# The first part of a LoRA-MoE layer with its operands swapped: tokens as TensorE's weights, 512 outputs streaming, results turned by VectorE and ScalarE

## The chip, the cores and the metric

The kernel runs on one NeuronCore of a Trainium2 chip. The metric is device time in microseconds, the median of several executions. Everything is fp32; the trace shows each fp32 matmul as two MATMUL instructions.

## What is computed

Eight sequences of 256 tokens with 1024 features go through three steps:

```python
w = cond_weight[ids]                                # one 1024 x 1024 matrix for each sequence
y = einsum('bsi,boi->bso', x, w)                    # part one
p = softmax(y @ router_W.T + router_b)              # 15 columns; the top 8 stay
w8 = sum of the kept p by expert_map                # 8 experts
h = y @ A.T                                         # 8 experts x rank 16 = 128 columns
out = x + (y @ base_W.T + base_b) + 2 * (h * w8) @ B
```

The matrix of a sequence differs from the next one's, so part one has eight products of 256 x 1024 by 1024 x 1024. Part two has one matrix, `base_W`, for all 2048 tokens.

## The kernel before

Both parts use the Winograd form of a 2 x 2 block product: seven block products in place of eight, and sums and differences of the blocks on VectorE.

**Part one** is a loop over the eight sequences `b`. The input of a sequence is cut into two halves of features (4 x 128 each) and two halves of tokens (128 each); its matrix into two halves of features and two of outputs (512 each). `load(b + 1)` brings the next sequence's tokens and the four quarters of its matrix (`a11`, `a12`, `a22`, `a21`, 1 MB each) with SP's queue into the tiles `x` and `wt` (eight buffers). VectorE makes the differences of the tokens in `turns` (`t1`, `t2`, `t4`), the sum `s1` in `first_sum`, and `s2`, a new `a21` and `s4` in `other_sums`, always for the next sequence, during the present one. TensorE runs seven blocks for each sequence: `a11`, `a12`, `s1`, `s2`, `a21`, `s4`, `a22` by their token blocks. A block is 16 matmuls of 128 x 128 weights, taken from the matrix, with 128 tokens streaming (`block`, L241). Its result lies in PSUM in `pa`, `pb` or `pc`, 2 buffers each, outputs on partitions and tokens along the free side. Some blocks accumulate on a bank that was read before (`s2` and `a22` on `pa`, `s4` on `pc`). ScalarE copies `pa` and `pc` out after their first use (L382, L394, L396) and takes the last block (L420); VectorE adds the others (L386, L408, L424). The results go straight into `ys`, where part two wants them: features on partitions, tokens along the free side.

Between the blocks of sequence `b` stands the routing of sequence `b - 1`: `project` (16 matmuls of 143 columns, L105), the softmax, the top 8 and the weights on VectorE (`weigh`), and `turn`, two TensorE transposes and a ScalarE copy that bring the weighted `h` into `hwTs`. After the loop the last `turn`, `project` and `weigh` follow.

`prepare_load(b)` loads a piece of `base_W` into `spare`; `prepare(b - 1)` makes the sums that part two needs (4 VectorE instructions for the first four pieces, 8 for the others) and writes them to DRAM (`left_raw`, `left_sum`). `load_left(n)` reads the left operands of product `n` of part two back. In the last iteration the order on SP is: `load_left` for the first product, `prepare(7)`'s two writes, `load_left` for the second product.

**Part two** takes the tokens in two groups of four sequences. Each group has seven outer products (`seven`), and each outer product is again seven blocks (`product`, L468), here 4 matmuls of 256 columns in a block, with the `up` terms of the LoRA part (L477) in four of the seven outer products. A queue of small VectorE steps (`soon`, `later`) is worked off between the blocks, two at a time. Group 0 is products 0 to 6, group 1 is products 7 to 13.

The order on TensorE, VectorE, ScalarE and SP is the order of the program text (`manual_schedule`). Every engine works through its instructions in that order.

Of the kernel before, what the change touches and what calls it, by code (L numbers as in the profile page):

```python
# [28 lines left out]
def kernel(  # L29
# [57 lines left out]

    ys = [
        ypool.tile([P, 2, 2, 2, 2, 2, S], F32, name=f"y{g}") for g in range(B // GB)
    ]  # L90
    hwTs = [const.tile([P, 2, 2, S], F32, name=f"hwT{g}") for g in range(B // GB)]
# [4 lines left out]
    def project(b, ar_sb, rpool, ps_h, order=(0, 1)):  # L96

        y = ys[b // GB]
        th, bi = b % GB // 2, b % 2
        h = rpool.tile([P, NTT, ER], F32, name="h")  # L100
        lg = rpool.tile([P, NTT, N], F32, name="lg")
        ph = ps_h.tile([P, NTT, ER + N], F32, name="ph")
        for j in order:
            for k in range(KC):
                nc.tensor.matmul(  # L105
                    ph[:, j],
                    lhsT=y[:, k // KH, th, k % KH // 2, bi, k % 2, ts(j, P)],
                    rhs=ar_sb[:, k, :],
                    start=(j == order[0] and k == 0),
                    stop=(k == KC - 1),  # L110
                    skip_group_check=True,
                )
        nc.scalar.copy(h, ph[:, :, :ER])  # L113
        nc.vector.tensor_add(  # L114
            lg, ph[:, :, ER:], rb.unsqueeze(1).to_broadcast([P, NTT, N])
        )
        mx = rpool.tile([P, NTT], F32, name="mx")
        nc.vector.tensor_reduce(mx, lg, AX.X, ALU.max)
        nc.vector.tensor_sub(lg, lg, mx.unsqueeze(2).to_broadcast([P, NTT, N]))
        ex = rpool.tile([P, NTT, N], F32, name="ex")  # L120
        nc.scalar.activation(ex, lg, AF.Exp)
        return h, ex

    def weigh(h, ex, route, rpool, hwpool):

        den = rpool.tile([P, NTT], F32, name="den")
        nc.vector.tensor_reduce(den, ex, AX.X, ALU.add)
        rden = rpool.tile([P, NTT], F32, name="rden")
        nc.vector.reciprocal(rden, den)
        pr = rpool.tile([P, NTT, N], F32, name="pr")  # L130
        nc.vector.tensor_mul(pr, ex, rden.unsqueeze(2).to_broadcast([P, NTT, N]))
        top = rpool.tile([P, NTT, 8], F32, name="top")
        rest = rpool.tile([P, NTT, N], F32, name="rest")
        for j in range(NTT):
            nc.vector.max(out=top[:, j, :], in_=pr[:, j, :])
        for j in range(NTT):
            nc.vector.match_replace(
                out=rest[:, j, :],
                in_to_replace=top[:, j, :],
                in_values=pr[:, j, :],  # L140
                imm_value=0.0,
            )

        kept = rpool.tile([P, NTT, N], F32, name="kept")
        nc.vector.tensor_sub(kept, pr, rest)
        w = rpool.tile([P, NTT, E], F32, name="w")
        for j in range(NTT):
            kr = rpool.tile([P, E, N], F32, name="kr")
            nc.vector.tensor_mul(
                kr, route, kept[:, j, :].unsqueeze(1).to_broadcast([P, E, N])  # L150
            )
            nc.vector.tensor_reduce(w[:, j, :], kr, AX.X, ALU.add)
        hw = hwpool.tile([P, NTT, ER], F32, name="hw")
        nc.vector.tensor_mul(
            hw.rearrange("p j (e r) -> p (j e) r", r=R),
            h.rearrange("p j (e r) -> p (j e) r", r=R),
            w.rearrange("p j e -> p (j e)").unsqueeze(2).to_broadcast([P, NTT * E, R]),
        )
        return hw
# [45 lines left out]
    with ExitStack() as phase:  # L205
        xpool = phase.enter_context(tc.tile_pool(name="x", bufs=2))
        mpool = phase.enter_context(tc.tile_pool(name="m", bufs=1))
        cpool = phase.enter_context(tc.tile_pool(name="c1", bufs=1))
        rpool = phase.enter_context(tc.tile_pool(name="route", bufs=2))
# [8 lines left out]

        em_f = cpool.tile([P, N], F32, name="em_f")
        route = cpool.tile([P, E, N], F32, name="route")  # L220

        def constants():
            nc.sync.dma_start(rb, router_b.to_broadcast([P, N]))
            nc.sync.dma_start(em_i, emap.to_broadcast([P, N]))
            nc.sync.dma_start(bb, base_b)
            nc.sync.dma_start(ar_sb.rearrange("p k n -> p (k n)"), ar)
            nc.vector.tensor_sub(bb[:, KH:], bb[:, KH:], bb[:, :KH])
            nc.vector.tensor_copy(em_f, em_i)
            for e in range(E):
                nc.vector.tensor_scalar(  # L230
                    route[:, e, :], em_f, float(e), SCALING, ALU.is_equal, ALU.mult
                )

        ar_sb = cpool.tile([P, KC, ER + N], F32, name="ar_sb")

        def block(acc, left, right, first, k_outer=False):
            order = [(m, k) for m in range(KH) for k in range(KH)]
            if k_outer:
                order.sort(key=lambda mk: mk[1])
            for n, (m, k) in enumerate(order):  # L240
                nc.tensor.matmul(  # L241
                    acc[:, m // 2, m % 2, :],
                    lhsT=left[:, k, ts(m, P)],
                    rhs=right[:, k, :],
                    start=(first and n == 0),
                    stop=(k == KH - 1),
                    skip_group_check=True,
                )

# [109 lines left out]
        waiting = None  # L359
        for b in range(B):  # L360
            last = b == B - 1

            def out(oh, th):
                return ys[b // GB][:, oh, b % GB // 2, :, b % 2, :, ts(th, P)]
# [10 lines left out]
            pa = ps.tile([P, 2, 2, P], F32, name="pa")  # L375
            pb = ps.tile([P, 2, 2, P], F32, name="pb")
            pc = ps.tile([P, 2, 2, P], F32, name="pc")
            m1 = mpool.tile([P, 2, 2, P], F32, name="m1")
            u2 = mpool.tile([P, 2, 2, P], F32, name="u2")
            m5 = mpool.tile([P, 2, 2, P], F32, name="m5")  # L380
            block(pa, q["a11"], b11, True, b == 0)
            nc.scalar.copy(m1, pa)  # L382
            if waiting:
                turn(*waiting)
            block(pb, q["a12"], b21, True, b == 0)
            nc.vector.tensor_add(out(0, 0), pb, m1)  # L386
            if b == 0:
                pd = ps.tile([P, 2, 2, P], F32, name="pb")
                block(pd, q["a22"], t4, True, True)
                nc.scalar.copy(out(1, 0), pd)  # L390
            if not last:
                nt1, nt2, nt4 = turns(x)
            block(pc, q["s1"], t1, True, b == 0)
            nc.scalar.copy(m5, pc)  # L394
            block(pa, q["s2"], t2, False)
            nc.scalar.copy(u2, pa)  # L396
            if b > 0:
                h, ex = project(b - 1, ar_sb, rpool, ps_h)
            if not last:
                first_sum(nq)  # L400
            if b == 0:
                block(pc, q["s4"], b22, False)
                block(pa, q["a21"], b12, False)
                nc.vector.tensor_add(out(1, 1), pa, m5)
                nc.vector.tensor_add(out(1, 0), pa, out(1, 0))
            else:
                block(pa, q["a21"], b12, False)
                nc.vector.tensor_add(out(1, 1), pa, m5)  # L408
                hw = weigh(h, ex, route, rpool, rpool)
                waiting = b - 1, hw  # L410
                block(pc, q["s4"], b22, False)
                if last:
                    nc.vector.tensor_add(out(0, 1), pc, u2)
                    left[0] = load_left(lefts[0])
                    terms = [step() for step in differences(ys[0][:, 0, 0])]
                    prepare(b)
                block(pa, q["a22"], t4, False)
                if last:
                    left[1] = load_left(lefts[1])
                nc.scalar.copy(out(1, 0), pa)  # L420
            if not last:
                other_sums(nq)
                q, t1, t2, t4 = nq, nt1, nt2, nt4
                nc.vector.tensor_add(out(0, 1), pc, u2)  # L424
# [5 lines left out]


        turn(*waiting)
        nh, nex = project(B - 1, ar_sb, rpool, ps_h, (1, 0))
        waiting = B - 1, weigh(nh, nex, route, rpool, const)

    with ExitStack() as phase:
# [3 lines left out]
        xpool = phase.enter_context(tc.tile_pool(name="x2", bufs=6))  # L443
        vpool = phase.enter_context(tc.tile_pool(name="v", bufs=1))
# [123 lines left out]
        for g in range(B // GB):  # L568
            y, hw = ys[g], hwTs[g]
# [3 lines left out]
            v = vpool.tile([P, 2, 2, 2, S], F32, name="v")  # L573
# [6 lines left out]
            def load_x(*r):  # L580
                xs[r] = xpool.tile([P, 2, S], F32, name="xt")
# [62 lines left out]
            for n, (right, base, into, done, *up_hw) in enumerate(seven):  # L644
# [5 lines left out]
                else:  # L650
                    follows = None if end else ys[g + 1][:, 0, 0]
# [25 lines left out]
                if end and n == 6:  # L677
# [4 lines left out]
                    )  # L682
                if here + 2 < len(lefts):
# [10 lines left out]
                if here == 0:  # L694
                    turn(*waiting)
# [65 lines left out]
```

## Time and profile before

| what | value |
|---|---|
| median of three runs | 442.53 us (442.32 to 443.61) |
| the profiled execution, its own time | 444.51 us |
| its span, first to last instruction | 442.7 us |
| TensorE busy (matmul) | 436.4 us, 99% |
| VectorE busy | 303.1 us, 68% |
| ScalarE busy | 40.3 us, 9% |
| mean granted TensorE clock | 0.996 |
| DMA | 106.19 MB, mean 240 GB/s |

The span is cut in time by the stages: part one's first block starts at 7.42 us, its last block ends at about 238.0 us, the turn and projection of sequence 7 end at 242.1 us, and part two runs from there to the end. A busy share is an average over stages that differ. A row of the timeline gives start, duration, engine, line, operation, output<-input, shapes and a count, and in brackets the idle time before it and what ended it. Matmul ends are modelled and overlap a little, so the time of a block is read from the start of one to the start of the next.

### The profile page before, as it was taken

The page shows a single profiled execution, that of the slowest core. Times are in us where ns is not written, and L with a number is a line of the kernel's source. Part 1 is how long each engine was busy: PE and PEld are TensorE (multiplying, and loading weights), DVE is VectorE, ACT ScalarE, POOL GpSimd, SP SyncE. Part 2 cuts the span into 40 slices and gives each one's busy share as a digit, 9 for nine tenths or more (in the row PEclk, how much of TensorE's full clock was granted, in tenths as well). Part 3 has the DMA queues.
Part 4 walks back from the last instruction along what each step waited for, and adds up shares of the span by engine and source line. Part 5 has one row for each costly group of instructions (what it writes and reads, how often), then busy time and mean ns, then how long its engine had stood idle before and what let it go on. Part 6 is the DMA issues. An engine that isn't in the chain of part 4 may idle for free.

```text
span 442.7 us, 7249 instructions
## 1 busy us (share of the span) xinstructions
PE 436.4 (99%) x2998; PEld 411.8 (93%) x2998; DVE 303.1 (68%) x516; ACT 40.3 (9%) x89; POOL 0.7 (0%) x6
## 2 busy tenths in 40 slices
PE   7999999999999999999999999999999999999997
PEld 6999999999999999999999888888888888888886
DVE  2678696582872976949719957756497867755594
ACT  1110101111011110110111200000200200000200
POOL 0000000000000000000000000000000000000000
PEclk8999999999999999999999999999999999999999
DMA  8997977668588777884280966730977726921843
GB/s 316 362 389 285 329 267 285 236 260 287 210 283 244 271 266 284 286 305 148 99 330 1 331 263 238 318 133 14 353 277 235 279 95 222 359 94 45 312 145 139
DMA packets 32786, 106.19 MB, mean 240 GB/s; under 512 B 3058, under 2 KB 6898, under 8 KB 29554
## 3 DMA queue, kind: packets, MB, share of 16 engines
q1 hardware_dynamic: 32466, 104.69, 65.0%
q10 hardware_dynamic: 288, 1.05, 0.6%
q8 instruction: 23, 0.38, 0.3%
q14 instruction: 9, 0.07, 0.0%
HBM read 84.49 MB, written 21.23 MB: 239 GB/s over the span
## 4 chain that ended last, share of the span: by engine, by line
PE 93%; DVE 5%; DMA 1%; issue 1%; SPq 0%
PE pa L241 25%; PE pa L468 20%; PE pc L241 12%; PE pc L468 10%; PE pb L241 7%; PE ph L105 6%; PE pb L468 5%; PE pc L477 3%; PE pb L477 2%; PE pa L477 1%; DMA wt<-in_wq_dram 1%; DVE tt L184 1%; PE pe L468 1%; DVE y L620 0%; PE pt L201 0%
## 5 line engine op out<-in xcount | busy, mean ns | idle before, releaser
L468 PE MATMUL pa<-tt,wt 128*128 128x256 f32 x324 | 78.0, 379 | 0.1
L468 PEld LDWEIGHTS pa<-tt,wt 128*128 128x128 f32 x324 | 61.4, 190 | 8.9 <-DVE u L498 0.5
L241 PE MATMUL pa<-x,wt 128*128 128x128 f32 x512 | 61.3, 280 | 1.9 <-DMA wt<-in_wq_dram 1.9
L241 PEld LDWEIGHTS pa<-x,wt 128*128 128x128 f32 x512 | 60.0, 196 | 2.0 <-issue 2.0
L241 PE MATMUL pa<-tt,wt 128*128 128x128 f32 x480 | 56.0, 275 | 0.0
L241 PEld LDWEIGHTS pa<-tt,wt 128*128 128x128 f32 x480 | 54.8, 192 | 0.0
L114 DVE TENSOR_TENSOR lg<-ph,rb 128x30 f32<-128x30 f32 x8 | 1.5, 188 | 50.1 <-ACT h L113 50.1
L105 PE MATMUL ph<-ar_sb,y 128*128 128x143 f32 x256 | 32.7, 284 | 0.0
L105 PEld LDWEIGHTS ph<-ar_sb,y 128*128 128x128 f32 x256 | 31.8, 190 | 0.0
L241 PE MATMUL pc<-tt,wt 128*128 128x128 f32 x256 | 29.9, 275 | 0.0
L241 PE MATMUL pb<-x,wt 128*128 128x128 f32 x256 | 29.9, 275 | 0.0
L241 PE MATMUL pc<-x,wt 128*128 128x128 f32 x256 | 29.9, 275 | 0.0
L241 PEld LDWEIGHTS pc<-tt,wt 128*128 128x128 f32 x256 | 29.2, 192 | 0.0
L241 PEld LDWEIGHTS pc<-x,wt 128*128 128x128 f32 x256 | 29.2, 192 | 0.0
L241 PEld LDWEIGHTS pb<-x,wt 128*128 128x128 f32 x256 | 29.2, 192 | 0.0
L468 PE MATMUL pc<-tt,wt 128*128 128x256 f32 x112 | 27.8, 379 | 0.0
L332 DVE TENSOR_TENSOR wt<-wt 128x2048 f32<-128x2048 f32 (+1 forms) x9 | 18.4, 2050 | 8.9 <-DMA wt<-in_wq_dram 8.8
L468 PE MATMUL pc<-y,wt 128*128 128x256 f32 x96 | 24.0, 379 | 0.0
L468 PE MATMUL pb<-y,wt 128*128 128x256 f32 x96 | 24.0, 379 | 0.0
L468 PEld LDWEIGHTS pc<-tt,wt 128*128 128x128 f32 x112 | 21.2, 190 | 3.0
L468 PE MATMUL pa<-y,wt 128*128 128x256 f32 x92 | 21.8, 379 | 0.0
L591 DVE TENSOR_TENSOR q<-q,xt 128x512 f32<-128x512 f32 x31 | 21.3, 686 | 0.5
(117 smaller groups left out, 489.0 us busy)
## 6 DMA issues: line engine op xcount, KB each, us to landing
wt<-in_wq_dram SPq DMA_DIRECT2D x28, 1024.0 KB, 5.1
wt<-left_raw SPq DMA_DIRECT2D x14, 1024.0 KB, 5.3
wt<-left_sum SPq DMA_DIRECT2D x14, 768.0 KB, 7.6
xt<-in_xr_dram SPq DMA_DIRECT2D x32, 256.0 KB, 6.4
out_dram<-q SPq DMA_DIRECT2D x31, 256.0 KB, 2.2
x<-in_xq_dram SPq DMA_DIRECT2D x7, 1024.0 KB, 4.8
wt<-in_wq_dram SPq DMA_DIRECT2D x8, 512.0 KB, 6.8
spare<-in_bq_dram SPq DMA_DIRECT2D x4, 1024.0 KB, 5.1
```

The lines of the kernel that those rows point to most:

```text
L105: nc.tensor.matmul(ph[:, j], lhsT=y[:, k // KH, th, k % KH // 2, bi, k % 2, ts(j, P)], rhs=ar_sb[:, k, :], start=(j == order[0] and k == 0 ...
L114: nc.vector.tensor_add(lg, ph[:, :, ER:], rb.unsqueeze(1).to_broadcast([P, NTT, N]))
L184: nc.vector.tensor_sub(t[n], x, y)
L241: nc.tensor.matmul(acc[:, m // 2, m % 2, :], lhsT=left[:, k, ts(m, P)], rhs=right[:, k, :], start=(first and n == 0), stop=(k == KH - 1), ...
L332: nc.vector.tensor_add(q["s1"][:, h], q["a21"][:, h], q["a22"][:, h])
L468: nc.tensor.matmul(acc[mi][:, mi, :], lhsT=left[:, 2 * k + mi, :], rhs=right[:, k, :], start=(first and k == 0 and (mi == 0 or acc[0] is n ...
L477: nc.tensor.matmul(acc[mi][:, mi, :], lhsT=up[:, ts(mi, P)], rhs=hw, start=False, stop=True, skip_group_check=True,)
L591: add(q, q, x)
```

## The change

In part one the two operands change places. A block is now 4 matmuls: 128 x 128 tokens are the weights, and 512 outputs of the matrix stream. The result of a block has tokens on partitions and 512 outputs along the free side, in four staging areas (`m0` for output half 0, `m1` for output half 1, two token halves each). To bring it into the layout of `ys`, `flip` has VectorE transpose each 128 x 512 piece in blocks of 32 x 32, and `moves` has ScalarE copy the blocks across partitions: 16 copies of 32 partitions x 256 elements for each of `m0` and `m1`. The copies of `m0` are issued after its second flip, the copies of `m1` at the start of the next sequence: eight before the copy of `pa`, eight after it (`behind`). The last 16 copies of sequence 7 lie between the blocks of part two's first product.

The block of `s4` now stands before `a21`, and `project` between `a21` and `a22`. `other_sums` stands after the routing steps, and the last flip, which reads `pa` directly in place of ScalarE's copy, after `other_sums`. `project` and `weigh` are one function that returns four steps. The projection of the last sequence is moved behind part two's second product, its `turn` behind the third; the `turn` of sequence 6 is behind the first product. In the last iteration `prepare(7)` is behind the last flip. Staging, routing values and the tile `v` of part two share one tile, `late`; four of the six `xt` places are the staging areas.

```diff
-    def project(b, ar_sb, rpool, ps_h, order=(0, 1)):
+    late = const.tile([P, 4 * OH + 2 * KC * S // 2 + 512], F32, name="late")
+    lo = 4 * OH
+    ms = late[:, :lo].rearrange("p (o h f) -> p o h f", o=2, h=2)
+    v = late[:, lo : lo + 8 * S].rearrange("p (i j k t) -> p i j k t", i=2, j=2, k=2)
...
+    def project(b, ph, order=(0, 1)):
...
+        return [logits, softmax, top, weigh], (b, hw)
...
-        def block(acc, left, right, first, k_outer=False):
-            order = [(m, k) for m in range(KH) for k in range(KH)]
-            if k_outer:
-                order.sort(key=lambda mk: mk[1])
-            for n, (m, k) in enumerate(order):
+        def block(acc, left, right, first):
+
+            for k in range(KH):
                 nc.tensor.matmul(
-                    acc[:, m // 2, m % 2, :],
-                    lhsT=left[:, k, ts(m, P)],
-                    rhs=right[:, k, :],
-                    start=(first and n == 0),
+                    acc,
+                    lhsT=right[:, k, :],
+                    rhs=left[:, k, :],
+                    start=(first and k == 0),
                     stop=(k == KH - 1),
                     skip_group_check=True,
                 )
+
+        def flip(half, of):
+
+            nc.vector.transpose(half, of)
+
+        def moves(b, oh, m):
+
+
+            y = ys[b // GB][:, oh, b % GB // 2, b % 2].rearrange(
+                "p q k (h a j) -> p (q k) h a j", h=2, a=4
+            )
+            m = m.rearrange("p h (q r j) -> p q h r j", q=KH, r=4)
+            return deque(
+                (
+                    lambda a=a, r=r: nc.scalar.copy(
+                        y[32 * r : 32 * r + 32, :, :, a, :], m[32 * a : 32 * a + 32, :, :, r, :]
+                    )
+                )
+                for r in range(4)
+                for a in range(4)
+            )
+
+        def run(steps, n=None):
+            for _ in range(len(steps) if n is None else min(n, len(steps))):
+                steps.popleft()()
...
-            block(pa, q["a11"], b11, True, b == 0)
-            nc.scalar.copy(m1, pa)
+            m0, m1 = ms[:, 0], ms[:, 1]
+            block(pa, q["a11"], b11, True)
+            run(behind, 8)
+            nc.scalar.copy(m0[:, 0], pa)
             if waiting:
                 turn(*waiting)
-            block(pb, q["a12"], b21, True, b == 0)
-            nc.vector.tensor_add(out(0, 0), pb, m1)
+            run(behind)
+            block(pb, q["a12"], b21, True)
+            nc.vector.tensor_add(m0[:, 0], pb, m0[:, 0])
+            flip(m0[:, 0], m0[:, 0])
...
-            block(pc, q["s1"], t1, True, b == 0)
-            nc.scalar.copy(m5, pc)
+            block(pc, q["s1"], t1, True)
+            nc.scalar.copy(m1[:, 1], pc)
             block(pa, q["s2"], t2, False)
-            nc.scalar.copy(u2, pa)
-            if b > 0:
-                h, ex = project(b - 1, ar_sb, rpool, ps_h)
+            nc.scalar.copy(m0[:, 1], pa)
             if not last:
                 first_sum(nq)
+            block(pc, q["s4"], b22, False)
+            nc.vector.tensor_add(m0[:, 1], pc, m0[:, 1])
+            flip(m0[:, 1], m0[:, 1])
+            run(moves(b, 0, m0))
+            block(pa, q["a21"], b12, False)
+            nc.vector.tensor_add(m1[:, 1], pa, m1[:, 1])
+            flip(m1[:, 1], m1[:, 1])
+            if last:
+                left[0] = load_left(lefts[0])
+                terms = [step() for step in differences(yv[0][:, 0, 0])]
             if b == 0:
-                block(pc, q["s4"], b22, False)
-                block(pa, q["a21"], b12, False)
-                nc.vector.tensor_add(out(1, 1), pa, m5)
-                nc.vector.tensor_add(out(1, 0), pa, out(1, 0))
+                nc.vector.tensor_add(m1[:, 0], pa, m1[:, 0])
+                flip(m1[:, 0], m1[:, 0])
+                other_sums(nq)
             else:
-                block(pa, q["a21"], b12, False)
-                nc.vector.tensor_add(out(1, 1), pa, m5)
-                hw = weigh(h, ex, route, rpool, rpool)
-                waiting = b - 1, hw
-                block(pc, q["s4"], b22, False)
-                if last:
-                    nc.vector.tensor_add(out(0, 1), pc, u2)
-                    left[0] = load_left(lefts[0])
-                    terms = [step() for step in differences(ys[0][:, 0, 0])]
-                    prepare(b)
+                ph = ps_h.tile([P, NTT, ER + N], F32, name="ph")
+                steps, waiting = project(b - 1, ph)
+                for step in steps:
+                    step()
                 block(pa, q["a22"], t4, False)
-                if last:
-                    left[1] = load_left(lefts[1])
-                nc.scalar.copy(out(1, 0), pa)
-            if not last:
-                other_sums(nq)
+                if not last:
+                    other_sums(nq)
+                flip(m1[:, 0], pa)
+            behind = moves(b, 1, m1)
+            if last:
+                prepare(b)
+                left[1] = load_left(lefts[1])
+            else:
                 q, t1, t2, t4 = nq, nt1, nt2, nt4
-                nc.vector.tensor_add(out(0, 1), pc, u2)
...
-        turn(*waiting)
-        nh, nex = project(B - 1, ar_sb, rpool, ps_h, (1, 0))
-        waiting = B - 1, weigh(nh, nex, route, rpool, const)
...
+                if here == 0:
+                    for k, count in enumerate((2, 1, 1, 4, 4, 3, 1)):
+                        gaps[k].append(lambda count=count: run(behind, count))
...
                 if here == 0:
+                    turn(*waiting)
+                elif here == 1:
+
+                    ph = ps_e.tile([P, 2, S], F32, name="pe")
+                    steps, waiting = project(B - 1, ph)
+                    soon.extend(steps)
+                elif here == 2:
                     turn(*waiting)
```

## The prediction

> **What bounds the kernel now.** I read the page's first two parts, then its chain, then the timeline of TensorE through one sequence.
>
> ```profile
> span 442.7 us, 7249 instructions
> PE 436.4 (99%) x2998; PEld 411.8 (93%) x2998; DVE 303.1 (68%) x516; ACT 40.3 (9%) x89; POOL 0.7 (0%) x6
> PEclk8999999999999999999999999999999999999999
> PE 93%; DVE 5%; DMA 1%; issue 1%; SPq 0%
> ...
> 66.63 0.38 PE L201 MATMUL pt<-ident,hw 128*128 128x128 f32 x2
> 66.85 3.74 PE L241 MATMUL pb<-x,wt 128*128 128x128 f32 x32
> 70.42 3.74 PE L241 MATMUL pc<-tt,wt 128*128 128x128 f32 x32
> ...
> 242.12 1.89 PE L468 MATMUL pa<-y,wt 128*128 128x256 f32 x8
> 243.85 1.89 PE L468 MATMUL pc<-tt,wt 128*128 128x256 f32 x8
> ```
>
> TensorE is the whole path, at full clock but for the start. A block of part one takes 3.57 us (66.85 to 70.42), 111.6 ns for each of 32 instructions; a sequence takes 7 x 3.57 + 0.22 (turn) + 3.92 (projection) = 29.15 us. ScalarE is idle 91% of the time and VectorE 32%, and their waits are for TensorE. So the question is what the change saves on TensorE, and whether the longer work on the other two makes TensorE wait.
>
> **What TensorE saves.** Part two's rows show 256 columns in (243.85 - 242.12) / 8 = 215.9 ns. 128 more columns cost 104 to 107 ns, so a fixed 2 to 5 ns goes with each instruction. 512 columns cost about 427 + 2.5 = 429 ns, a block of 8 takes 3.43 us: 0.14 us less. 56 blocks save 7.7 us at most, 1.7%. The number of columns that stream is the same; only the fixed part shrinks.
>
> **What the others get.** For each sequence ScalarE gets 32 copies of 32 x 256 and loses one of 512; VectorE gets four flips of 128 x 512. Their costs:
>
> ```profile
> L394 ACT COPY m<-pc 128x512 f32<-128x512 f32 x8 | 4.7, 586 | 48.6 <-PE pc L241 48.6
> L113 ACT COPY h<-ph 128x256 f32<-128x256 f32 x8 | 3.0, 372 | 26.4 <-PE ph L105 26.4
> 245.77 0.23 ACT L121 ACTIVATE ex<-lg 128x30 f32<-128x30 f32 x1 [0.83 <-DVE lg L119]
> 245.91 0.82 ACT L507 ACTIVATE u<-pc,bb 128x256 f32<-128x256 f32 x2
> ```
>
> A copy: 256 to 512 elements adds 214 ns, so streaming 256 elements takes 214 ns and that is the floor. The Exp reads SBUF, takes 228 ns for 30 elements, 203 ns beyond streaming, so a copy from SBUF lasts about 0.41 us; the next instruction starts 0.14 us after the Exp, 90 ns before its end. If copies overlap like that, one follows another every 0.31 to 0.33 us. [...] Both ends stay for the range; I take 0.31, because the Exp row shows the overlap.
>
> A flip: the nearest row is a VectorE add of 128 x 512, 0.69 us, and I take 0.70. [...]
>
> Sums of busy time do not decide: 32 x 0.31 = 10 us on ScalarE and 2.8 us on VectorE would fit into 28 us. The order decides.
>
> **The new loop.** Four places tie the engines together. The last flip stands on VectorE behind `other_sums`, which stands behind the routing, which waits for the projection. The eight copies of `m1` at the head of the next sequence wait for that flip. The copy of `pa` stands on ScalarE behind these eight. The block of `s2` accumulates on `pa` and waits for that copy; then come `s4`, `a21` and the next projection. The pieces, from the trace:
>
> ```profile
> 110.65 3.73 PE L241 MATMUL pa<-x,wt 128*128 128x128 f32 x32
> 110.85 0.37 ACT L113 COPY h<-ph 128x256 f32<-128x256 f32 x1 [3.29 <-PE ph L105]
> 111.25 0.19 DVE L114 TENSOR_TENSOR lg<-ph,rb 128x30 f32<-128x30 f32 x1 [8.06 <-ACT h L113]
> 111.92 0.23 ACT L121 ACTIVATE ex<-lg 128x30 f32<-128x30 f32 x1 [0.70 <-DVE lg L119]
> ...
> 115.03 0.17 DVE L127 TENSOR_REDUCE den<-ex 128x2 f32<-128x30 f32 x1
> 117.99 2.29 DVE L337 TENSOR_TENSOR wt<-wt 128x2048 f32<-128x2048 f32 x1
> 124.59 0.68 DVE L424 TENSOR_TENSOR y<-pc,u 128x512 f32<-128x512 f32 x1
> ```
>
> Projection ends (110.65) to Exp's end: 1.50. Softmax to weighted h: 117.99 - 115.03 = 2.96. `other_sums`: 124.59 - 117.99 = 6.60. Flip 0.70. Eight copies 8 x 0.31 = 2.5, copy of `pa` 0.59, hand-overs between engines about 0.12. Then TensorE: three blocks 10.30, projection 3.92. Sum 29.2 us for a sequence, against 29.15 before and 28.2 if TensorE never waited. Each sequence from 2 on has TensorE wait about 1 us ahead of `s2`, and what the block saves is gone. A second loop runs over the 16 copies of `m0`, which stand ahead of the copy of `h`: 18.5 + 32 copies, 28.4 at 0.31 us; it takes over from 0.35 us on.
>
> `first_sum` must be done when `s4` ends. It waits for the load of `a21`, issued at the end of the `s1` block (landing 6.1 to 6.3 us in most sequences, 8.2 in one) and takes 2.3: 8.6 us after `s1`, while two blocks and the wait take 8.1. That is hidden by the 16 copies, which end before the projection.
>
> Sum up to the end of part one: sequence 0 (six blocks) and 1 (seven) keep their gain, -1.8; on entering the loop 16 copies that are late for `first_sum` cost once about 0.7; six rounds of 29.2 cost +0.3; two rounds in which `prepare` has eight steps (5.4 us where four take 2.0) put `first_sum` late by 0.3 each. Together -0.2: no gain, no loss.
>
> **The seam between the parts.** Before, the second product's left operands came just in time:
>
> ```profile
> 243.64 0.37 SPq L277 DMA_DIRECT2D left_raw<-spare  x1
> 244.24 0.37 SPq L277 DMA_DIRECT2D left_sum<-spare  x1
> 244.66 1.21 SPq L164 DMA_DIRECT2D wt<-left_raw  x1
> 245.92 1.23 SPq L168 DMA_DIRECT2D wt<-left_sum  x1
> ...
> 254.78 1.89 PE L468 MATMUL pa<-y,wt 128*128 128x256 f32 x8
> ```
>
> The load of 244.66 took 9.8 us to land, at 254.5; its product began at 254.78. It stands on SP behind the two writes of `prepare(7)`. With the change `prepare(7)` stands behind the last flip, and the projection that lay ahead of the first product (3.92 us of cover) stands after the second. Count from E, the end of the last block of part one (238.0 before). VectorE has five steps of `differences` ahead of the routing: the routing begins 0.85 us after the projection, weighted h is ready at 5.4 (one more step lies inside), the flip ends at 6.1, which is E + 2.7. Ahead of the first write lie seven steps of `prepare` (4.9 us, from 212.66 to 217.59 in the earlier iteration) and, by the order of the changed program, three part-two updates at 0.61: E + 9.5. The load lands 10.9 us after that write is issued, as before: E + 20.4. The first product and the turn end at E + 12.3. TensorE waits 8.1 us for it, some 3 us of it already inside the first product, where `a22` waits for a VectorE add that is queued behind the same steps. The two loads behind it have the rest of the second product and the projection as cover.
>
> A wait of about 5 us in one piece can also lower the clock. The trace shows it once: the first block took 5.27 us (7.42 to 12.69) where 3.57 is usual, in the slice with PEclk 8. [...] I take half, 0.9.
>
> The first product's operands stand on SP behind `prepare(6)`'s writes, whose steps began 3.8 us after the start of sequence 7 (212.66 against 208.83) and now begin when the flip ends, at 8.4: 4.6 later. They landed by 231.9, 6.1 us ahead of E, so 1.5 us of cover stay. If that is gone, it costs what is missing, up to 3 us. The loads into the four staging areas (`xt`) wait for the last copies; they are first needed late in the second product. The first block of sequence 0 takes its operands in the same half loads, k by k, as before. ScalarE's lost copy (L420) was not on the path.
>
> Everything else in part two has the same TensorE work, and its 0.1 us waits; the 4 us routing of sequence 7 moves to where VectorE has idle time. Taken as free; if VectorE is full there, up to 2 us.
>
> **Sum.** -0.2 + 8.1 + 0.9 = +8.8 us on a span of 442.7. The profiled execution took 444.51, 1.8 beyond its span and 2.0 above the median; set on the median, 442.53 + 8.8 = 451.3.
>
> **Rivals.**
> - *TensorE's saving comes through (faster).* For: 0.14 us a block is certain, ScalarE has room. Against: even at the floor of 0.214 us a copy the loop takes 26.7 + 8 x 0.214 = 28.4, so part one gains 5 us at most; and the seam must lose under 5. It decides if the load lands in the 5.3 us that is the page's median for such loads and no part-two step stands ahead of `prepare(7)`'s write: E + 2.7 + 4.9 + 1.0 + 5.3 = 13.9, a wait of 1.6, total about 439. Chance 0.10.
> - *Copies don't overlap.* Their start partitions change with each copy and nothing in the trace does that. At 0.41 us the second loop takes 18.5 + 13.1 = 31.6, by walking the queues 31.1: part one +11, seam and clock +9, 462. Chance 0.20.
> - [...] Both loops grow by one or two flips, the eight-step rounds to 31.2, entering costs more: part one +8, total 461. Chance 0.10; with slow copies too, 473, chance 0.05.
> - *The main case*, 450 to 453, chance 0.55 with its neighbours between 445 and 457.
>
> A measurement of this kernel can tell about 0.3%, 1.3 us, from no change. Faster 0.08 (the first rival but for its slow edge), within it 0.05 (that edge, and a main case with a hidden seam), slower 0.87. The range reaches from the floor of the copies (445) over both single rivals on the slow side (465); it leaves out the faster case and the doubled one.
>
> **What would show it.** Right: 224 matmuls of 128 x 512 (448 instructions, near 429 ns each in a block); TensorE waiting about 1 us ahead of each `s2` for ScalarE's copy of `pa`; copies 0.31 us apart; a hole of 5 to 8 us about 12 us into part two, ended by the DMA of `left_raw`. Wrong: blocks of `s2` without a wait and rounds of 28.2; copies 0.4 apart with waits ahead of `s4`, too; the second product starting on time.

## The result and the profile after

The changed kernel takes 474.84 us (median of 6, 474.05 to 476.2), the kernel before 442.71 (median of 6, 442.32 to 443.61): 1.0727 times as long, 95% interval 1.0707 to 1.0747. That is 32.1 us more; the prediction had 8.8 more, and 474.84 lies above its range of 445 to 465. The profiled execution took 474.13 us, its span is 472.4.

The page of the changed kernel (span, busy TensorE, granted clock, chain, and the row of the 256 new copies: busy us, mean ns of one, idle time before them):

```profile
span 472.4 us, 4836 instructions
...
PE 439.0 (93%) x1654; PEld 297.1 (63%) x1654; DVE 326.7 (69%) x548; ACT 139.1 (29%) x338; POOL 0.7 (0%) x6
...
PEclk9999998999999999999989989999999999999999
...
PE 55%; DVE 17%; ACT 16%; DMA 6%; issue 6%; SPq 0%; DVEq 0%; ACTq 0%
...
L294 ACT COPY y<-late 32x256 f32<-32x256 f32 x256 | 103.0, 402 | 111.0 <-DVE late L283 108.1
```

TensorE fell from 99% of the span to 93%, and the chain, once 93% TensorE, is now a third VectorE and ScalarE. ScalarE is still idle 71% of the time: its busy share shows nothing of this loss. One round of the loop, from the timeline of all engines:

```profile
120.35 6.61 ACT L294 COPY y<-late 32x256 f32<-32x256 f32 x16 [4.84 <-DVE late L283]
...
126.99 0.37 ACT L152 COPY late<-ph 128x256 f32<-128x256 f32 x1
...
130.96 0.42 DVE L193 TENSOR_TENSOR late<-late 128x256 f32<-128x256 f32 x1
131.30 2.28 DVE L393 TENSOR_TENSOR wt<-wt 128x2048 f32<-128x2048 f32 x1
...
137.91 0.71 DVE L283 STREAM_TRANSPOSE late<-pa 128x512 f32<-128x512 f32 x1
...
138.65 3.31 ACT L294 COPY y<-late 32x256 f32<-32x256 f32 x8 [10.36 <-DVE late L283]
...
141.98 0.59 ACT L436 COPY late<-pa 128x512 f32<-128x512 f32 x1
...
142.62 2.84 PE L272 MATMUL pa<-wt,tt 128*128 128x512 f32 x6 [2.54 <-ACT late L436]
```

Read it downwards. Sixteen copies of `m0` last 6.61 us, 0.413 each, with no overlap. The copy of the routing's `h` stands behind them on ScalarE and starts when they end, at 126.99, though its projection ended about 125.97. The softmax and the weights follow (to 130.96), then the three sums of `other_sums`, the flip at 137.91, eight more copies (3.31 us), the copy of `pa`, and only then may `s2` start, 2.54 us late (six of its eight instructions lie in this view). Each step of this chain waits for the data of the one before it or stands behind it in a queue.

The seam, from the timeline of TensorE and from that of SP:

```profile
254.80 3.60 PE L272 MATMUL pa<-wt,tt 128*128 128x512 f32 x8
261.42 1.97 PE L526 MATMUL pa<-y,wt 128*128 128x256 f32 x8 [3.03 <-issue]
...
277.53 3.57 PE L526 MATMUL pa<-y,wt 128*128 128x256 f32 x8 [3.32 <-DMA wt<-left_raw]
280.93 1.03 PE L526 MATMUL pc<-tt,wt 128*128 128x256 f32 x4
...
306.37 1.99 PE L526 MATMUL pa<-tt,wt 128*128 128x256 f32 x8 [0.64 <-DVE u L556]
```

```profile
267.76 0.37 SPq L333 DMA_DIRECT2D left_raw<-spare  x1
...
268.78 1.22 SPq L206 DMA_DIRECT2D wt<-left_raw  x1
```

Part one ends at 254.80 + 3.43 = 258.23. The first product waits 3.19 us, the second 3.48, a later block 0.64; the block at 277.53 takes 3.40 us where 1.73 is usual, at a mean granted clock of 0.53. The rounds are read from the starts of the `turn` on TensorE, here four of the changed kernel and, last, one of the kernel before:

```profile
67.24 0.38 PE L243 MATMUL pt<-ident,late 128*128 128x128 f32 x2
...
132.83 0.38 PE L243 MATMUL pt<-ident,late 128*128 128x128 f32 x2
...
164.57 0.38 PE L243 MATMUL pt<-ident,late 128*128 128x128 f32 x2
...
228.99 0.38 PE L243 MATMUL pt<-ident,late 128*128 128x128 f32 x2
```

```profile
212.40 0.38 PE L201 MATMUL pt<-ident,hw 128*128 128x128 f32 x2
```

Three of the five rounds take 31.74 us like the one from 132.83 to 164.57; the other two take 33.85 and 32.68. Set beside the kernel before:

| stretch | before | after | difference |
|---|---|---|---|
| start to the first turn | 66.63 | 67.24 | +0.6 |
| five rounds, turn to turn | 145.77 | 161.75 | +16.0 |
| last turn to the end of part one | 25.6 | 29.2 | +3.7 |
| from there to the end of the span | 204.7 | 214.2 | +9.5 |

The sum is the difference of the spans, 29.7 (rounded). The medians lie 32.1 apart because the profiled execution of before was 1.8 us slower than its median and that of after 0.7 faster. Most of the 1.8 lies in its first block, 5.27 us where 3.57 is usual, at a mean granted clock of 0.68 behind a wait of 1.86 us. Over the whole profiled execution of before the mean clock is 0.996, over those beside the experiments 0.999 to 1.0. Against such an execution the start lost about 2.3 us and not 0.6.

### The profile page after: what moved, and what is told of

It is laid out like the page before. It is cut to its first block, busy times and chain, and to the rows that moved or that the text cites. A ratio compares the mean times of both kernels' runs of the same rounds, so it can differ in the third digit from the quotient of the medians.

```text
span 472.4 us, 4836 instructions
## 1 busy us (share of the span) xinstructions
PE 439.0 (93%) x1654; PEld 297.1 (63%) x1654; DVE 326.7 (69%) x548; ACT 139.1 (29%) x338; POOL 0.7 (0%) x6
## 4 chain that ended last, share of the span: by engine, by line
PE 55%; DVE 17%; ACT 16%; DMA 6%; issue 6%; SPq 0%; DVEq 0%; ACTq 0%
PE pa L526 19%; ACT y L294 14%; PE pc L526 9%; PE pa L272 7%; PE pc L272 6%; PE pb L526 4%; DVE wt L393 3%; DVE wt L401 3%; DMA wt<-in_wq_dram 3%; PE pc L535 3%; DMA wt<-left_raw 2%; DVE late L283 2%; PE pb L535 1%; PE pb L272 1%; PE pa L535 1%
## 5 line engine op out<-in xcount | busy, mean ns | idle before, releaser
L294 ACT COPY y<-late 32x256 f32<-32x256 f32 x256 | 103.0, 402 | 111.0 <-DVE late L283 108.1
L272 PE MATMUL pa<-wt,tt 128*128 128x512 f32 x120 | 61.4, 661 | 18.9 <-ACT late L436 18.9
L526 PEld LDWEIGHTS pa<-tt,wt 128*128 128x128 f32 x324 | 61.2, 190 | 10.0 <-DVE u L556 1.7
L272 PE MATMUL pa<-wt,x 128*128 128x512 f32 x128 | 57.7, 593 | 1.5 <-DMA wt<-in_wq_dram 1.5
L272 PEld LDWEIGHTS pa<-wt,x 128*128 128x128 f32 x128 | 24.2, 190 | 32.2 <-issue 31.1
L139 PEld LDWEIGHTS ph<-late,y 128*128 128x128 f32 x224 | 28.4, 189 | 3.3 <-issue 3.3
L272 PE MATMUL pc<-wt,x 128*128 128x512 f32 x64 | 29.1, 597 | 1.5 <-ACT late L450 1.5
L272 PE MATMUL pb<-wt,x 128*128 128x512 f32 x64 | 28.8, 592 | 0.0
L272 PE MATMUL pc<-wt,tt 128*128 128x512 f32 x64 | 28.8, 592 | 0.0
L139 PE MATMUL ph<-late,y 128*128 128x143 f32 x224 | 28.6, 284 | 0.0
L388 DVE TENSOR_TENSOR wt<-wt 128x2048 f32<-128x2048 f32 (+1 forms) x9 | 18.5, 2055 | 14.6 <-DMA wt<-in_wq_dram 13.0
L526 PEld LDWEIGHTS pc<-tt,wt 128*128 128x128 f32 x112 | 21.3, 190 | 3.0
```

What stands on the lines that cost most here:

```text
L139: nc.tensor.matmul(ph[:, j, : ER + N], lhsT=y[:, k // KH, th, k % KH // 2, bi, k % 2, ts(j, P)], rhs=ar_sb[:, k, :], start=(j == order[0] ...
L272: nc.tensor.matmul(acc, lhsT=right[:, k, :], rhs=left[:, k, :], start=(first and k == 0), stop=(k == KH - 1), skip_group_check=True,)
L294: lambda a=a, r=r: nc.scalar.copy(y[32 * r : 32 * r + 32, :, :, a, :], m[32 * a : 32 * a + 32, :, :, r, :])
L388: nc.vector.tensor_add(q["s1"][:, h], q["a21"][:, h], q["a22"][:, h])
L526: nc.tensor.matmul(acc[mi][:, mi, :], lhsT=left[:, 2 * k + mi, :], rhs=right[:, k, :], start=(first and k == 0 and (mi == 0 or acc[0] is n ...
```

## The experiments

Theory A: a ScalarE copy overlaps the one before it only if both start in the same partitions; so the copies cost 0.41 and not 0.31 us, and the loop over ScalarE and VectorE grows to 31.7. Theory B: the place of one instruction in its queue is at fault (the flip behind `other_sums`), not the price of the copies. Theory C: the lowered clock (a mean of 0.981 over the changed kernel's profiled execution, 0.996 before) carries a good part of the loss.

### The spacing of the copies by their start partitions

Each sequence's copies take another pattern of source and target partitions. The blocks land in other places than part two expects.

```diff
-                    lambda a=a, r=r: nc.scalar.copy(
-                        y[32 * r : 32 * r + 32, :, :, a, :], m[32 * a : 32 * a + 32, :, :, r, :]
-                    )
+                    lambda a=a, r=r: one(b, y, m, a, r)
...
+        def one(b, y, m, a, r):
+            to, of, w = {
+                0: (0, 0, 32), 1: (0, a, 32), 2: (r, 0, 32), 3: (r, a, 32),
+                4: (a, a, 32), 5: (0, 0, 128), 6: (r, r, 32), 7: (r, a, 32),
+            }[b]
+            nc.scalar.copy(
+                y[32 * to : 32 * to + w, :, :, a, :], m[32 * of : 32 * of + w, :, :, r, :]
+            )
```

> The changed kernel, with the copies of ScalarE taking other partitions in each sequence, so the results land in wrong places (GpSimd clears ys first): sequence 0 copies always from partition 0 to partition 0; 1 changes the source alone; 2 the target alone; 3 and 7 change both, as in the changed kernel; 4 has source and target equal and changing with each copy; 5 copies 128 partitions from 0 to 0; 6 has source and target equal, changing every four copies. Theory A (a copy that starts in another quarter of the partitions than the one ahead of it waits for its end): 0.31 to 0.32 us from one copy to the next in sequences 0 and 5, nearly so in 6, 0.41 in 1, 2 in part, 3, 4 and 7. Theory B (copies from SBUF to SBUF never overlap on ScalarE): 0.41 us in all of them.

One execution, 477.28 us. ScalarE's timeline, groups of 16 copies of sequences 1, 2, 3 and 5 (start, us for the 16):

```profile
61.11 6.81 ACT L299 COPY y<-late 32x256 f32<-32x256 f32 x16 [9.82 <-DVE late L286]
...
93.81 5.32 ACT L299 COPY y<-late 32x256 f32<-32x256 f32 x16 [4.39 <-DVE late L286]
...
125.82 6.61 ACT L299 COPY y<-late 32x256 f32<-32x256 f32 x16 [6.91 <-DVE late L286]
...
190.66 5.00 ACT L299 COPY y<-late 128x256 f32<-128x256 f32 x16 [4.84 <-DVE late L286]
```

One start everywhere gives 5.00 us for 16 copies, a spacing of 0.306 when the last copy's 0.40 is allowed for. The source alone changing with each copy gives 0.425, the pattern of the change 0.413. A change with every fourth copy (6, and 2, where only the target changes) gives 5.31 and 5.32: three copies of 16 pay about 0.1 more each. 128 partitions or 32 make no difference (24 copies of 32 partitions with one start, in sequence 0, take 7.45 us, a spacing of 0.307). So a copy whose source or target starts in another quarter of the partitions (32 each) than that of the one before it begins only 0.41 to 0.425 us after it, when that one, 0.40 us long in the changed kernel, has ended: 0.10 to 0.12 us for each change. Why, these runs don't show. Both prices of the prediction exist; the kernel has the dear one, and no order avoids it, as each of the 16 copies has another pair of quarters.

### The same kernel with copies that start alike

All 128 partitions are copied in each instruction, 256 elements a partition as before, so every copy starts at partition 0. The blocks aren't moved across partitions.

```diff
-                        y[32 * r : 32 * r + 32, :, :, a, :], m[32 * a : 32 * a + 32, :, :, r, :]
+                        y[:, :, :, a, :], m[:, :, :, r, :]
```

> The changed kernel with every copy of ScalarE taking all 128 partitions from 0 to 0 (the same 256 elements on each), so blocks aren't moved across partitions and ys is wrong; the number of copies, their places in the queues and what waits for them are the same. Copies should follow each other every 0.306 us. Theory: the prediction's sum was right but for this one duration; rounds of 29.2 to 29.6 us with a wait of about 1 us ahead of s2, full clock in part one, 451 to 454 us. Rival (the sum missed another cost of 2 us a round): rounds stay above 30.5 us, over 460 us.

461.67 us, 1.0439 times before (1.0422 to 1.0457): 13.2 us of the 32.1 are gone, and it is still 8 us above what was expected. TensorE's timeline:

```profile
127.23 0.38 PE L243 MATMUL pt<-ident,late 128*128 128x128 f32 x2
...
135.31 3.70 PE L272 MATMUL pa<-wt,tt 128*128 128x512 f32 x8 [0.82 <-ACT late L436]
...
156.50 0.38 PE L243 MATMUL pt<-ident,late 128*128 128x128 f32 x2
...
166.13 5.40 PE L272 MATMUL pa<-wt,tt 128*128 128x512 f32 x8 [2.38 <-ACT late L436]
...
189.02 0.38 PE L243 MATMUL pt<-ident,late 128*128 128x128 f32 x2
```

The round from 127.23 to 156.50 takes 29.27 us with a wait of 0.82 ahead of `s2`: the prediction's loop (29.2, about 1). Three of the five rounds are like that. The one after it takes 32.52. Its cause, from VectorE's timeline:

```profile
142.82 2.29 DVE L388 TENSOR_TENSOR wt<-wt 128x2048 f32<-128x2048 f32 x1 [3.47 <-DMA wt<-in_wq_dram]
...
155.37 0.42 DVE L193 TENSOR_TENSOR late<-late 128x256 f32<-128x256 f32 x1
```

`first_sum` waits 3.47 us for the load of `a21`. The flip, the 16 copies, the copy of `h` and the routing behind it are late, too: the weighted `h` starts 1.13 us ahead of its turn, 2.69 (186.33 to 189.02) in the round after. The 1.56 between them is the growth of the wait ahead of `s2`, 0.82 to 2.38, and the block behind that wait takes 5.24 us (166.13 to 171.37) where 3.43 is usual, another 1.8, in a slice of the page (160.2 to 171.7) with PEclk 8. Another round (66.59 to 97.97) takes 31.38, its turn and its `s2` late in the same way, behind a wait of 2.41 us for such a load.

### The flip ahead of `other_sums`

```diff
                 block(pa, q["a22"], t4, False)
+                flip(m1[:, 0], pa)
                 if not last:
                     other_sums(nq)
-                flip(m1[:, 0], pa)
```

> The changed kernel with the last flip of each sequence ahead of other_sums on VectorE. Theory: the loop flip, 16 copies ahead of the copy of pc, s4, second flip, 16 copies, copy of h, routing, other_sums sets the round, 18.5 + 32 x 0.41 = 31.7 us; without the 6.6 us of other_sums it is 25.1, TensorE's own 28.2 us decides, the waits of 2.5 to 3.7 us ahead of s2 go, and with them the halved clock. Rounds of 28.2 to 29.3 us, 446 to 450 us in all. Rival (ScalarE is simply too slow, whatever the order): rounds stay above 31 us, under 8 us gained.

470.11 us, 1.0634 (1.0601 to 1.0667), 4.7 us less than the changed kernel and 20 more than expected. Theory B fails in this form: the waits ahead of `s2` are gone from sequence 2 on, but TensorE waits at the `turn` instead, 1.3 to 3.4 us. The five rounds together are 3.6 us shorter and the end of part one 4.5; the seam is 3.0 longer, with blocks of 3.40 and 3.58 us, where 1.73 is usual, behind its two waits of 3.02 and 3.49 (mean clock of the execution 0.978). Timeline of all engines:

```profile
148.41 2.29 DVE L388 TENSOR_TENSOR wt<-wt 128x2048 f32<-128x2048 f32 x1 [3.69 <-DMA wt<-in_wq_dram]
...
152.08 6.61 ACT L294 COPY y<-late 32x256 f32<-32x256 f32 x16 [9.06 <-DVE late L283]
...
158.71 0.37 ACT L152 COPY late<-ph 128x256 f32<-128x256 f32 x1
...
163.24 0.41 PE L243 MATMUL pt<-ident,late 128*128 128x128 f32 x2 [3.20 <-DVE late L193]
```

A third loop takes over at about 31.5 us a round: turn, two blocks, load of `a21`, `first_sum`, flip, 16 copies, copy of `h`, routing, turn. It shares the 16 copies with the other one. The loops must be cut where they meet, at the copy of `h` behind the 16 copies.

### The copy of `h` ahead of the 16 copies

With the flip moved as above, the copies of `m0` stand behind the routing steps in sequences 1 to 6:

```diff
-            run(moves(b, 0, m0))
+            if b == 0 or last:
+                run(moves(b, 0, m0))
...
                 for step in steps:
                     step()
+                if not last:
+                    run(moves(b, 0, m0))
```

> The kernel with the flip ahead of other_sums, and ScalarE's copy of h and its Exp ahead of the 16 copies of m0 (not in the last sequence). Theory: what held that kernel at rounds of 31.5 us is a third loop: turn, two blocks, the load of a21 (9 us there), first_sum, the second flip, 16 copies, copy of h, routing, turn. Without the 16 copies in it TensorE's own 28.2 us decides: no wait at turn, rounds of 28.2 to 28.6 us, 445 to 449 us. Rival (VectorE or the load of a21 is the bound): rounds stay at 30 to 31.5 us, 460 us and more.

450.19 us, 1.0191 (1.0138 to 1.0244): 24.7 us less than the changed kernel, with every copy still 0.413. TensorE's timeline:

```profile
123.70 0.38 PE L243 MATMUL pt<-ident,late 128*128 128x128 f32 x2
...
151.87 0.38 PE L243 MATMUL pt<-ident,late 128*128 128x128 f32 x2
```

The rounds are 28.17 us, TensorE's own work without a wait. Waits are left in sequence 1 (2.94 us) and at the seam (3.02, 2.36 and 0.63), which puts it 1 us above the range expected. The copy's move was run only together with the flip's.

### The left operands ahead of `prepare(7)`

```diff
             if last:
-                prepare(b)
                 left[1] = load_left(lefts[1])
+                prepare(b)
```

> The changed kernel with the load of the second product's left operands ahead of the two writes of prepare(7) on SP. Theory: the wait of 3.5 us ahead of the second product of part two goes, and the block of 3.4 us at half clock behind it takes 1.7 again: 5 us less, 469 to 470 us. The wait of 3 us ahead of the first product stays, because that one is for the flip that reads pa. Rival (the load is late because its buffers or the DMA engines are busy): under 1.5 us gained.

470.88 us, 1.0617 (1.0592 to 1.0642): 4 us less. The second product starts without a wait. The 3.02 us at the first product stay, and now two slow blocks follow them (mean clock of the execution 0.978). TensorE's timeline:

```profile
261.72 3.75 PE L526 MATMUL pa<-y,wt 128*128 128x256 f32 x8 [3.02 <-issue]
265.26 3.09 PE L526 MATMUL pc<-tt,wt 128*128 128x256 f32 x8
```

Those two blocks take 3.54 and 2.93 us instead of 1.73. In the changed kernel the same wait of 3.03 us had no such result (1.81 and 1.72 us, at a granted clock of 1.00), and the slow block, at 0.53, came behind the next one, of 3.32.

### TensorE's swap by itself

The kernel before with its operands swapped in `block` and nothing else; results land in a layout that part two doesn't expect.

```diff
...
-                    acc[:, m // 2, m % 2, :],
-                    lhsT=left[:, k, ts(m, P)],
-                    rhs=right[:, k, :],
+                    acc,
+                    lhsT=right[:, k, :],
+                    rhs=left[:, k, :],
...
```

> The kernel before with the operands of a block swapped and nothing else: 4 matmuls of 512 columns where 16 of 128 stood, the results left unturned, so what lies in ys is wrong. This is the gain of the swap by itself. Theory: 3.43 us for a block where it was 3.57, 56 blocks, 7.7 us less: 435 us, no new waits. Rival (the longer block holds its bank longer, or the token weights load later): waits of VectorE or TensorE in part one, less than 5 us gained.

435.48 us, 0.9831 (0.9815 to 0.9848): 7.5 us less than the 443.01 of before in these runs. TensorE's timeline:

```profile
63.23 3.60 PE L239 MATMUL pb<-wt,x 128*128 128x512 f32 x8
66.67 3.60 PE L239 MATMUL pc<-wt,tt 128*128 128x512 f32 x8
```

The 0.14 us a block is real, and all the rest of the change costs 39 us on top.

### Filling the waits with matmuls

Twelve idle 128 x 128 matmuls ahead of each `s2` keep TensorE busy while it would wait.

```diff
+            if b > 0:
+                busy = ps_h.tile([P, NTT, ER + N], F32, name="ph")
+                for _ in range(12):
+                    nc.tensor.matmul(
+                        busy[:, 0, :P], lhsT=ident, rhs=ident, start=True, stop=True
+                    )
             block(pa, q["s2"], t2, False)
```

> The changed kernel with 12 matmuls of 128 x 128 on the identity, into the idle bank of the projection, between the blocks s1 and s2 of sequences 1 to 7: TensorE works through the first 2.6 us of its wait. Theory: the waits themselves stay, the halved clock behind four of them goes: four times 1.8 us, 467 to 468 us. Rival (the clock is lowered for another reason, or the filler makes the block late): 474 us or more.

473.98 us, 1.0689 (1.0644 to 1.0735): 0.9 us less than the changed kernel, with intervals that overlap, and 6 us above what was expected. Theory C fails for part one. TensorE's timeline:

```profile
142.98 3.70 PE L272 MATMUL pa<-wt,tt 128*128 128x512 f32 x8
147.18 3.70 PE L272 MATMUL pc<-wt,x 128*128 128x512 f32 x8 [0.49 <-ACT late L450]
```

Part one has no block of 5.23 us any more (mean clock 0.993 against 0.981), and four of the five rounds take 31.73 to 31.81. The loop over ScalarE and VectorE sets the round, and a slow `s2` block lies partly beside it. In the changed kernel it takes the place of the wait of 0.50 us ahead of `s4`, and the round with the slow block of 174.37 is 0.94 us longer than the others (32.68 against 31.74), not 1.8. The expectation had counted each slow block in full.

### A version without the loops

The copy of `h` first and the left operands first, as above (the latter's lines are not shown again). In the last sequence the flip of `pa` also stands ahead of the routing's last step:

```diff
-                for step in steps:
+                for step in steps[:3]:
                     step()
                 if not last:
                     run(moves(b, 0, m0))
+                    steps[3]()
                 block(pa, q["a22"], t4, False)
                 flip(m1[:, 0], pa)
-                if not last:
+                if last:
+                    steps[3]()
+                else:
                     other_sums(nq)
```

> The last one, and at the seam the load of the second product's left operands ahead of prepare(7)'s writes and the last flip ahead of the last two routing steps. Theory: rounds of 28.2 to 28.6 us, no wait ahead of the second product, about 1 us in place of 3 ahead of the first, full clock: 437 to 441 us, faster than the kernel before. Rival: prepare(7) and the updates that part two queues on VectorE still hold the first product by 3 us and lower the clock: 443 to 446 us.

442.94 us, 1.0006 (0.9997 to 1.0015): level with before, and 2 us above the range expected. Four losses are left. Three are at the seam (0.91, 1.52 and 0.63 us; at the latter two VectorE was busy without a gap). The largest is in sequence 1, from ScalarE's and from TensorE's timeline:

```profile
34.87 9.95 ACT L294 COPY y<-late 32x256 f32<-32x256 f32 x24 [9.62 <-DVE late L283]
44.84 0.58 ACT L436 COPY late<-pa 128x512 f32<-128x512 f32 x1
```

```profile
45.48 5.40 PE L272 MATMUL pa<-wt,tt 128*128 128x512 f32 x8 [3.68 <-ACT late L436]
```

Twenty-four copies in one go, late because VectorE in sequence 0 first waits 2.43 us for the load of `a21` and makes the sum. `s2` waits 3.68 us behind them and then takes 5.23 us (45.48 to 50.71) where 3.43 is usual.

### `first_sum` behind the flip in sequence 0

On top of the last version:

```diff
-            if not last:
+            if 0 < b < B - 1:
                 first_sum(nq)
...
             flip(m0[:, 1], m0[:, 1])
+            if b == 0:
+                first_sum(nq)
```

> The reordered kernel (flip of pa's half first, left loads first, copy of h ahead of the routing's copies out of the way) had one large stall left in part one: in its sequence 1 ScalarE ran 24 copies in one go from 34.87 to 44.84 us before the copy of pa that s2 waits for (3.68 us), and the gap cost one block at half clock (5.23 instead of 3.43 us). Those copies started late because VectorE, in sequence 0, stood 2.43 us at first_sum for the load of a21 and made the sum (2.29 us) before it turned the first half. Here only that order is changed: in sequence 0 first_sum comes after the turn. Theory: the turn ends near 29.5 us instead of 34.8, the copy of pa is done by 41.5 us, about when the block ahead of s2 ends; no wait, no half clock, 442.9 - 3.7 - 1.8 = 437.4 us, range 436.5 to 439, faster than both kernels. Rival: the second turn of the sequence (pa's half, still behind first_sum) holds the copies instead, and the wait ahead of s2 or of s4 stays at 2 us or more: 440 to 443 us.

438.9 us against 442.96 of before (medians of 5 and 9), 0.9906 (0.989 to 0.9922), at the upper end of the expected range: the first complete version that is faster than both kernels, by 0.9% against before. Page, and TensorE's timeline:

```profile
PE 428.5 (98%) x1654; PEld 295.2 (68%) x1654; DVE 325.0 (74%) x548; ACT 138.7 (32%) x338; POOL 0.7 (0%) x6
```

```profile
229.39 1.99 PE L534 MATMUL pa<-y,wt 128*128 128x256 f32 x8 [0.91 <-DVE late L283]
...
241.54 1.99 PE L534 MATMUL pa<-tt,wt 128*128 128x256 f32 x8 [1.52 <-DVE u L564]
```

Part one has no wait for a copy or a turn left. The waits at the seam (0.91, 1.52 and 0.64, together 3.1) account for most of the 3.4 us by which this is above the swap by itself. The same 256 copies and 32 flips as in the changed kernel are in it. Where they stand now they cost next to nothing. So neither the price of a copy nor the order of the queues is the cause alone: with cheap copies the changed kernel's order still loses, and with another order the dear copies fit in.

## Why the prediction was wrong

The direction held, and the kind of loss: TensorE's gain is real, and a loop through VectorE and ScalarE eats it. The size was 3.6 times too small. The step that failed first is the spacing of the copies, taken as 0.31 us and measured as 0.413: with it the second loop, not the first, sets the round, at 31.74 us and not 29.2. The second step that failed is `first_sum`, taken as hidden. Up to the end of part one the changed kernel lost 20.3 us where the prediction had -0.2; the seam came out near its sum. By its steps:

- *TensorE's saving* (0.14 us a block, 7.7 us at most): right. Blocks without a wait take 3.43 us, and the swap alone gives 7.5.
- *"I take 0.31, because the Exp row shows the overlap"*: the step that failed first. It measured 0.413. With copies at 0.306 the kernel is 13.2 us faster. The prediction saw the reason ("start partitions change with each copy and nothing in the trace does that") and took the value of a row that doesn't change them. The 0.41 us worked out there from the same row for the length of a copy agrees with the measured 402 ns.
- *The second loop, "18.5 + 32 copies"*: right in its result, though the prediction doesn't work out the 18.5. At 0.413 it gives 31.7; the rounds took 31.74 where nothing else came in. *The first loop, 29.2*: the 29.27 of the run with copies that start alike.
- *The rival "Copies don't overlap", part one +11*: its mechanism is what happened, its sum wasn't. It took 31.1 for the round. The five rounds alone lost 16.0, of which 5 x (31.74 - 29.15) = 13.0 is the loop and 3.1 two rounds that were longer still (33.85 and 32.68). The end of part one lost 3.7 more, a wait ahead of `s2` and a slow block in sequence 7.
- *`first_sum` "is hidden by the 16 copies", and entering the loop costs 0.7*: wrong. These copies have the copy of `h`, and so the next loop, behind them. With cheap copies two rounds still lost 2.1 and 3.3 us, the latter to a wait of 3.47 for the load; part one came to +6.4 where -0.2 was expected. In the changed kernel sequence 1 lost more than 4 us to a wait of 2.52 for the copy of `pa` and a block of 5.24 us at a mean granted clock of 0.67. Why the load lands later in some sequences isn't settled.
- *The seam, 8.1 + 0.9*: 9.5 measured, by another split, so that the sum comes this near is in part luck: waits of 3.19, 3.48 and 0.64 and a block 1.7 us longer at a granted clock of 0.53. The first product's wait came from the flip, which still read the bank of `pa` (flip at 260.61, product at 261.42; in the last run above the wait is shorter, and the trace puts it down to the flip); the prediction had `a22` wait later. The first write was issued at 267.76, 9.5 us after the end of part one, as computed. The second product started 19.3 us after the end of part one instead of 20.4.
- *Flip 0.70*: 0.71 measured. That flips could take much longer, the rival of 461, was the author's estimate, which no trace showed.
- *The 0.9 for the clock, at the seam only*: half of the 1.7 us of one slow block, behind a wait of 1.86 and not of 5; what a longer wait does was the author's estimate. In part one four more blocks took 5.23 or 5.24 us, at a mean granted clock of 0.67. The run with idle matmuls was rid of them and gained 0.9 us, which the noise covers.
- *1.5 us of cover on the first product's operands*: they were in time; the bank was the limit.

The range failed because its slow side ended at single mishaps (461, 462, and 473 at 0.05), and here the slow copies came together with the late sums and the seam. That 474.84 lies near the 473 is chance: that case needed flips much longer than the 0.71 measured.

## What to carry to other kernels

Moving work to an idle engine costs what it puts behind itself in that engine's queue: walk each loop through all queues, and list what stands behind each long group. Where a price depends on a condition that the trace never shows (here, start partitions that change), take the dear end until it is measured. When one loop is cut, the next one can be within a few tenths of a microsecond (here 31.5 behind 31.74): look for the instruction that they share, here the copy of `h` behind 16 copies, whose move on top of the flip's brought 20 us where the flip's had brought 4.7.

## What the hardware showed that was not expected

A ScalarE copy of 256 elements follows another after 0.306 us, and after 0.41 to 0.425 us when its source or target starts in another quarter of the partitions.

The lowered clock doesn't follow from the length of a gap alone. TensorE's timeline of the changed kernel:

```profile
142.62 3.70 PE L272 MATMUL pa<-wt,tt 128*128 128x512 f32 x8 [2.54 <-ACT late L436]
...
238.78 5.40 PE L272 MATMUL pa<-wt,tt 128*128 128x512 f32 x8 [2.54 <-ACT late L436]
```

Here gaps of 2.54 us (2.70 when counted from the block starts) led to a block of 5.23 us at 238.78, at a mean granted clock of 0.67, and to one of 3.48 us at 142.62, at 1.00 (in the slow block of 174.37 the granted clock was 0.50 from 176.2 to 178.0). In the run with copies that start alike a block of 5.24 us followed a gap of 2.38 us, and one of 3.53 a gap of 2.92. What else decides, the runs don't show.
